# Layer 0 of a two-layer transformer step: layer-norm and turning of rows by pairs of tiles, row sums tied to the end of a head group, and a new order of three small steps

## The chip, the cores and the metric

The kernel runs on one core of a Trainium2 chip. The metric is the time of one execution in device microseconds (us); smaller is better. The engines are named as the profile names them: PE (matrix multiplication), PEld (its weight loads), DVE (vector), ACT (activation), POOL (the general engine), SP (here only an issuer of DMAs). Every engine runs its own list of instructions in the order in which the program has them, and waits on semaphores for the others.

## The reference

Eight sequences of 512 rows of 512 float32 numbers go through two layers. Cut to what matters here:

```python
x = layernorm(x + attention0(x))     # 16 heads of 32, causal, with biases
x = layernorm(x + experts(x))        # 8 experts, top 2 of a softmax router, low-rank additions to all weights
x = layernorm(x + attention1(x))     # 8 heads of 64, 2 groups of keys and values, RMS-scaled input
x = layernorm(x + ffn(x))            # 1408 hidden, integer weights with scales

def layernorm(x, eps=1e-5):
    return (x - mean(x)) / sqrt(var(x) + eps)

# the router of the experts
probs = softmax(x @ (gate_w + 2 * lora_B @ lora_A).T)
weights, selected = top_k(probs, 2);  weights = weights / weights.sum(-1)
```

## The kernel before

**Layer 0 (the first 650 us).** `attention0` loops over the batches `b` (the eight sequences), in each over four groups `g` of four heads, and in each over three units `u` of keys (key tile 0; tiles 1 and 3; tile 2). One step `(g, u)` multiplies scores (`sc`), takes their exponential on ACT (`p`, L1573), masks the diagonal block on POOL (`select`, L1583), and one step later multiplies by the values (`av`, L1612) and adds up `p` on DVE (L1620). The sums of `p` are multiplied by ones (`rs`), inverted, and `normalise` writes `aoT` (L1634).

**Work laid between the steps.** `plan(b)` gives each step `(g, u)` a list `todo`, which runs between the scores and the product, and a list `late`, which runs after the product:

- queries and keys of the next group (`query`, `key`);
- for the batch before, `pb = b - 1`: `project(pb, t)` for four tiles of rows, with the addition to `x` out of the bank (L1495), statistics (L200, L201), then the norm of four tiles (L205) with their four stores into the router's rows (SP, L208);
- for `pb` from 0 to 5 (`by_dma`): `blocks(pb)`, which transposes 32x32 blocks of the four normed tiles on DVE (L108), writes them to DRAM in four DMAs (`turns.out`, L113) and reads them back in one (`turns.back`, L116); the result `x1T` is what the router's logits multiply (`score`, at step (3, 2); L515), after which `choose` picks two experts of each row;
- for `b + 1`: the values in seven products of half-size blocks instead of eight (`ps_1of` to `ps_7of`, in the order 1, 6, 2, 5, 3, 7, 4; the last one is in the plan of the next batch), whose results DVE adds up (L1437). Some of them need differences of blocks of x, four additions over 128x512 in all, made by `row_sums` on DVE (L806), from the transposed x that SP loads into `experts` (`load_xT`, L1373).

**Merging.** Beside this the low-rank additions are merged into the experts' weights: at the third unit of a group SP loads two pieces of weights (`merged<-in_gate_up` or `merged<-in_down`, L853), POOL adds the scaled product to each in the next two units (L855), and SP stores them (L856). The loading of `x` and `xT` for the next batch and the merging in the last group are put behind the return `x1T<-turned` in the program (`behind_return`).

**What sets the order.** Within layer 0 a list scheduler orders the instructions of every engine by their dependences and its own costs; `tc.issue_after(i)` keeps what is built under it behind instruction `i`. In the last two groups of the last batch, PE's order is the program's own. In the program that comes out, the orders on SP and POOL are plain lists, and a DMA or an addition that waits holds up everything behind it on its queue.

**Banks.** The PSUM (the memory of matmul results) gives four banks to `sc`, two to `av` and two, tag `mm`, to everything else in layer 0: queries, keys, projections, seven-products, `rs`, logits and rank.

**The change of layer.** Before layer 1 the experts' tiles run on PE with pieces of the first attention of layer 1 laid between them: `first_pieces` of `Attention1`, whose last three are the key, the value and the first query.

Of the kernel before, what the change touches and what calls it, by code (L numbers as in the profile page):

```python
# [9 lines left out]
F32 = mybir.dt.float32  # L10
# [4 lines left out]
ALU = mybir.AluOpType  # L15
# [3 lines left out]
P = 128  # L19
# [3 lines left out]
NT = S // P  # L23
# [5 lines left out]
LN_EPS = 1e-5  # L29
# [407 lines left out]
class Router:  # L437
# [80 lines left out]
    def choose(self, b, parts, ps, columns):  # L518

        nc, small = self.nc, self.small  # L520
        here = slice(NT * b, NT * (b + 1))

        def bc(a):
            return a[:, :, None].to_broadcast([P, NT, E])

        for t in range(NT):
            matmul_by_columns(nc, ps[:, t, :], parts[:, ts(t, P)], self.gather, columns=columns)
        pr = small.tile([P, NT, E], F32, name="pr")
        tmp = small.tile([P, NT, E], F32, name="tmp")
        top = small.tile([P, NT], F32, name="top")  # L530
        second = small.tile([P, NT], F32, name="second")
        red = small.tile([P, NT], F32, name="red")
        total = small.tile([P, NT], F32, name="total")
        nc.vector.tensor_reduce(red, ps, AX.X, ALU.max)
        nc.vector.tensor_tensor(tmp, ps, bc(red), ALU.subtract)
        nc.scalar.activation(tmp, tmp, AF.Exp)
        nc.vector.tensor_reduce(red, tmp, AX.X, ALU.add)
        nc.vector.reciprocal(red, red)
        nc.vector.tensor_tensor(pr, tmp, bc(red), ALU.mult)

        def first_of_largest(values, largest, one_hot):
            nc.vector.tensor_reduce(largest, values, AX.X, ALU.max)
            nc.vector.tensor_tensor(tmp, values, bc(largest), ALU.is_equal)
            nc.vector.tensor_tensor(tmp, tmp, self.iota, ALU.mult)
            nc.vector.tensor_reduce(red, tmp, AX.X, ALU.min)
            nc.vector.tensor_tensor(one_hot, self.iota, bc(red), ALU.is_equal)

        first_of_largest(pr, top, self.hots[:, 0, here, :])

        rest = small.tile([P, NT, E], F32, name="rest")  # L550
        nc.vector.scalar_tensor_tensor(rest, self.hots[:, 0, here, :], -2.0, pr, ALU.mult, ALU.add)
        first_of_largest(rest, second, self.hots[:, 1, here, :])
        nc.vector.tensor_tensor(total, top, second, ALU.add)
        nc.vector.reciprocal(total, total)
        nc.vector.tensor_tensor(self.weights[:, 0, here], top, total, ALU.mult)
        nc.vector.tensor_tensor(self.weights[:, 1, here], second, total, ALU.mult)


        self.both = small.tile([P, NT, E], F32, name="both")
        nc.vector.tensor_tensor(self.both, self.hots[:, 0, here, :], self.hots[:, 1, here, :], ALU.add)  # L560
        self.earlier = small.tile([P, NT, E], F32, name="earlier")
        nc.vector.tensor_copy(self.earlier[:, 0, :], self.carry)
        for t in range(1, NT):
            nc.vector.tensor_tensor(self.earlier[:, t, :], self.earlier[:, t - 1, :], self.both[:, t - 1, :], ALU.add)
        nc.vector.tensor_tensor(self.carry, self.earlier[:, NT - 1, :], self.both[:, NT - 1, :], ALU.add)

    def dispatch(self, b, ps, columns):

# [242 lines left out]
class Experts:  # L811
# [9 lines left out]
    def room(self, at, n):  # L821

        return self.w[:, at : at + n * 512].rearrange("p (u f) -> p u f", f=512)
# [510 lines left out]
def attention0(env, guard, keep, routes, experts, dram, p_mm, tiles_ctx):  # L1334
# [4 lines left out]
    tc, nc, ins, xs, vec = env.tc, env.nc, env.ins, env.xs, env.vec  # L1339
# [4 lines left out]
    with ExitStack() as phase:  # L1344
# [47 lines left out]
        router = Router(env, keep, routes, small, work, dram)  # L1392
# [29 lines left out]
        def row_sums(b):  # L1422
            return seven_of_rows(nc, xts[b], t_x)

        def seven(b, n):
            x_of, _ = row_sums(b)
            room = v_rooms[b % 2]
            ps = mm([P, 2, 256], f"ps_{n}of7")
            for s in range(2):
                for k in range(2):  # L1430
                    matmul_by_columns(nc, ps[:, s, :], x_of[n][:, k, ts(s, P)], v_of[n][:, k, :], start=k == 0, stop=k == 1)

            def block(i, j):
                return room[:, 2 * j : 2 * (j + 1), 256 * i : 256 * (i + 1)]

            def add(out, a):
                nc.vector.tensor_tensor(out, ps, a, ALU.add)  # L1437

            if n == 1:
                nc.scalar.copy(block(0, 0), ps)  # L1440
            elif n == 6:
                add(block(1, 0), block(0, 0))
            elif n == 2:
                add(block(0, 0), block(0, 0))
            elif n == 5:
                add(block(1, 1), block(1, 0))
            elif n == 3:
                add(block(0, 1), block(1, 1))
            elif n == 7:
                add(block(1, 1), block(1, 1))  # L1450
                add(block(1, 0), block(1, 0))
            else:
                add(block(1, 0), block(1, 0))
# [37 lines left out]
        def project(b, t, out_of_heads=False):  # L1491
            ps = mm([P, D], "ps_o")
            for c in range(ND):
                (wide if out_of_heads else multiply)(ps, aoTs[b][:, c, ts(t, P)], wo[:, c, :], c)
            nc.vector.tensor_tensor(xs[b][:, t, :], ps, xs[b][:, t, :], ALU.add)  # L1495
            if t == NT - 1:
                env.layernorm(b, lambda t: router.rows[router.row_at(b, t) :][:P])

        x1Ts, logits = {}, {}

# [1 line left out]
        turns = Turn(env, dram, NT, "turned0")  # L1502
        returned = [None]
# [4 lines left out]
        def room(b):  # L1508
            x1Ts[b] = work.tile([P, ND, S], F32, tag="x1T", name="x1T")

        def blocks(b):
            room(b)
            flat = x1Ts[b].rearrange("p k s -> p (k s)")
            for t in range(NT):
                turns.blocks(flat, t, xs[b][:, t, :])
            turns.out(flat)
            returned[0] = turns.back(flat)

        def turn(b, c, mm=mm):
            if c == 0:  # L1520
# [119 lines left out]
        merging, inverses, normed = {}, [], [None]  # L1640
# [6 lines left out]
        def plan(b):  # L1647

            todo, late = ({(g, u): [] for g in range(ND) for u in range(len(UNITS))} for _ in range(2))
# [8 lines left out]
            pb, last = b - 1, b == NB - 1  # L1658
            by_dma = 0 <= pb < by_blocks
# [5 lines left out]
            if b:  # L1665
                places = ((1, 0), (1, 1), (1, 2), (2, 0)) if by_dma else ((1, 0), (1, 0), (1, 1), (1, 1) if last else (1, 2))
                for t, slot in enumerate(places):
                    todo[slot].append(lambda t=t: project(pb, t))
                if by_dma:
                    todo[2, 1].append(lambda: blocks(pb))  # L1670
                else:
                    for c in range(ND):
                        at = todo[2, 1] if last and c >= 2 else (late if last else todo)[2, 0]
                        at.insert(c % 2 if at is todo[2, 1] else len(at), lambda c=c: turn(pb, c))
                todo[(3, 2) if by_dma else (2, 1)].append(lambda: score(pb))
                if not by_dma:
                    todo[(3, 0) if last else (2, 2)].append(lambda: choose(pb))
            if b == 0:
                todo[1, 0].append(lambda: router.merge_lora(mm([P, ND, E], "ps_wr")))
            if b + 1 < NB:  # L1680
                for slot, last_sums in (((0, 2), False), ((1, 0), True)) if b else (((2, 1), False), ((2, 2), True)):
                    late[slot].append(lambda last_sums=last_sums: row_sums(b + 1)[1](last_sums))
                for n, slot in zip(ORDER, ((1, 0), (2, 0), (2, 1), (2, 2), (3, 0), (3, 2)) if b else
                                   ((3, 0), (3, 0), (3, 1), (3, 1), (3, 2), (3, 2))):
                    todo[slot].append(lambda n=n: seven(b + 1, n))
# [14 lines left out]
        tiles = Tiles(env, router, experts.w, dram)  # L1700
# [22 lines left out]
        for b in range(NB):  # L1723
            todo, late = plan(b)
# [41 lines left out]
        b = NB - 1  # L1766
# [28 lines left out]
class Attention1:  # L1795
# [83 lines left out]
    def first_pieces(self):  # L1879

        do = self.first = self.prepare(0)

        def fetch(t):
            do["fetch"](t)
            self.scale(t)

        def blocks(tiles):
            for t in tiles:
                do["blocks"](t)

        return ([lambda t=t: fetch(t) for t in range(NT)] + [lambda t=t: do["add"](t) for t in range(NT)]
                + [do["deviations"], do["norm"], lambda: blocks((0, 1)), lambda: blocks((2, 3)), lambda: None, lambda: None]
                + [do["key"], do["value"], lambda: do["query"](0)])

    def scale(self, c):

# [554 lines left out]
```

## Time and profile before

| | |
|---|---|
| time, median of 3 runs | 2086.05 us (2085.02 to 2086.63) |
| the profiled execution's own time | 2084.99 us |
| its span, first to last instruction | 2083.3 us |
| granted PE clock over the span | 0.998 |
| PE busy | 2058.4 us (99%) |
| DVE, ACT, POOL busy | 1264.3, 645.3, 510.7 us |
| layer 0's attention, to the first matmul of the experts | about 654 us |

The span is what the rows of the profile cover; 1.7 us of the execution lie around it. A row of the timeline gives the start in us, the time that the group of equal instructions took, the engine, the line, the operation, out<-in, shapes, the count, and in brackets how long the engine had been idle and what ended that. An SP row is an issue of a DMA, not its landing. PE's times overlap, as matmuls are pipelined, so that a start is a surer number than an end.

### The profile page before, as it was taken

To read this page: it belongs to the slowest core of one execution; us is meant where nothing else is said; L and a number is where in the kernel's file an instruction comes from. 1 tells how busy PE (TensorE), PEld (TensorE's weight loads), DVE (VectorE), ACT (ScalarE), POOL (GpSimd) and SP (SyncE) were. 2 spreads that over 40 slices of the span, in tenths; PEclk is the share of its full clock that TensorE was granted. 3 is DMA by queue.
4 is the path that set the end of the run, shared out by engine and by line. 5 is a ranking of instruction groups with operands and counts; after the bars stand their busy time and mean duration, and the time that the engine had idled before them with its cause. 6 is when DMAs were issued, how large, how long until landed. Compare 5 with 4: busy or idle time off the path is not lost. (4 is left out here: it accounts for less than half of the span.)

```text
span 2083.3 us, 37551 instructions
## 1 busy us (share of the span) xinstructions
PE 2058.4 (99%) x15778; PEld 1069.4 (51%) x15778; DVE 1264.3 (61%) x2047; ACT 645.3 (31%) x916; POOL 510.7 (25%) x509
## 2 busy tenths in 40 slices
PE   9999999999999999999999999999999999999998
PEld 2333333333334677764433333333335888888886
DVE  3667687686777533233158889887868644455444
ACT  2444434344344111111143333333332322222222
POOL 1344444444435121221052231232101000000000
PEclk9999999999999999999999999999999999999999
DMA  6023424415334488876432332223102311111000
GB/s 208 22 83 123 143 81 145 150 63 173 107 139 177 153 222 256 245 228 187 129 102 62 112 122 71 77 96 102 41 1 71 101 41 61 61 61 61 21 21 22
DMA packets 193059, 226.10 MB, mean 109 GB/s; under 512 B 73818, under 2 KB 139610, under 8 KB 189298
## 3 DMA queue, kind: packets, MB, share of 16 engines
q1 hardware_dynamic: 180240, 185.44, 28.3%
q0 software_dynamic: 10560, 34.61, 5.7%
q10 hardware_dynamic: 2082, 3.56, 0.6%
q8 instruction: 127, 2.08, 0.4%
q14 instruction: 50, 0.41, 0.1%
HBM read 138.88 MB, written 84.69 MB: 107 GB/s over the span
## 5 line engine op out<-in xcount | busy, mean ns | idle before, releaser
L1573 ACT ACTIVATE p<-sc 128x2048 f32<-128x2048 f32 (+1 forms) x96 | 152.4, 1587 | 175.8 <-PE sc L67 175.8
L1262 DVE SCALAR_TENSOR_TENSOR hT<-ps_u,vec,sg 128x512 f32<-128x512 f32 x88 | 65.6, 745 | 189.4 <-PE ps_u L1257 189.1
L1583 POOL TENSOR_SCALAR_AFFINE_SELECT p<-p 128x512 f32<-128x512 f32 x128 | 97.2, 771 | 307.6 <-ACT p L1573 302.0
L1273 PE MATMUL ps_f<-ffn_w,h_half 128*128 128x512 f32 x664 | 167.6, 393 | 2.8 <-DVE h_half L1268 2.0
L990 PE MATMUL ps_gu<-xrT,experts 128*128 128x256 f32 x736 | 166.6, 379 | 0.0
L1110 POOL TENSOR_TENSOR g_total<-g_total,r_inv 128x512 f32<-128x512 f32 x64 | 83.7, 1308 | 316.2 <-DVE r_inv L2007 270.6
L1620 DVE TENSOR_TENSOR p<-p 128x1536 f32<-128x1536 f32 (+2 forms) x96 | 147.8, 1539 | 17.7 <-POOL x L1593 10.0
L990 PEld LDWEIGHTS ps_gu<-xrT,experts 128*128 128x128 f32 x736 | 139.3, 190 | 35.9 <-issue 19.3
L1977 ACT ACTIVATE p<-sc 128x1024 f32<-128x1024 f32 x128 | 124.2, 1022 | 100.5 <-PE sc L67 99.2
L2007 DVE RECIPROCAL r_inv<-r_inv 128x512 f32<-128x512 f32 x32 | 107.1, 3347 | 71.6 <-ACT r_inv L1107 71.6
L1273 PEld LDWEIGHTS ps_f<-ffn_w,h_half 128*128 128x128 f32 x664 | 122.9, 188 | 34.5 <-DVE h_half L1268 7.4
L1257 PE MATMUL ps_g<-x_high,ffn_w 128*128 128x512 f32 x352 | 137.2, 390 | 0.0
L1257 PE MATMUL ps_g<-x_low,ffn_w 128*128 128x512 f32 x352 | 137.0, 389 | 0.0
L1257 PE MATMUL ps_u<-x_low,ffn_w 128*128 128x512 f32 x352 | 136.9, 389 | 0.0
L1257 PE MATMUL ps_u<-x_high,ffn_w 128*128 128x512 f32 x352 | 136.9, 389 | 0.0
L67 PE MATMUL ps_q<-experts 128*32 128x512 f32 x1024 | 120.1, 603 | 6.1 <-DMA experts<-in_xT 4.3
L67 PE MATMUL sc<-qT,kT 64*64 64x512 f32 x1024 | 124.7, 602 | 1.2 <-ACT qT L1871 0.9
L1260 ACT ACTIVATE sg<-ps_g,vec 128x512 f32<-128x512 f32 x88 | 60.6, 689 | 195.6 <-PE ps_g L1257 195.6
L1996 PE MATMUL av<-p,v 128*64 128x512 f32 x512 | 120.8, 593 | 0.0
L202 POOL TENSOR_SCALAR rstd<-mv 128x4 f32<-128x4 f32 x15 | 3.9, 262 | 461.9 <-DVE mv L201 461.9
L67 PE MATMUL ps_k<-experts 128*32 128x512 f32 x1024 | 116.4, 595 | 0.0
L67 PE MATMUL ps_o<-attn_out,aoT 128*64 128x512 f32 x512 | 116.4, 598 | 0.0
(310 smaller groups left out, 3419.2 us busy)
## 6 DMA issues: line engine op xcount, KB each, us to landing
results<-y SPq DMA_DIRECT2D x68, 256.0 KB, 2.6
pair<-xrT SPq DMA_DIRECT2D x30, 512.0 KB, 3.3
xrT<-pair SPq DMA_DIRECT2D x120, 128.0 KB, 3.9
turned<-turned SPq DMA_DIRECT2D x56, 256.0 KB, 4.1
merged<-merged SPq DMA_DIRECT2D x48, 256.0 KB, 2.4
experts<-merged SPq DMA_DIRECT2D x8, 1536.0 KB, 6.6
x<-in_x SPq DMA_DIRECT2D x8, 1024.0 KB, 8.4
merged<-in_gate_up SPq DMA_DIRECT2D x32, 256.0 KB, 3.9
```

Source lines behind the costliest of these rows:

```text
L67: nc.tensor.matmul(out[m], lhsT=lhsT[:, m], rhs=rhs, start=start, stop=stop)
L990: nc.tensor.matmul(ps[:, j, :], lhsT=w, rhs=xT[:, c, :], start=c == 0, stop=c == ND - 1)
L1110: self.nc.gpsimd.tensor_tensor(self.total, self.total, r_inv, ALU.add)
L1257: nc.tensor.matmul(ps, lhsT=w[:, ts(dc, P)], rhs=x[:, dc, :], start=(dc, i) == (0, 0), stop=(dc, i) == (ND - 1, 1))
L1262: nc.vector.scalar_tensor_tensor(hT, u, vec[:, V_SU + c : V_SU + c + 1], sg, ALU.mult, ALU.mult)
L1273: self.nc.tensor.matmul(os[t], lhsT=h[:, ts(t, P)], rhs=self.weights(2 * NHID + c), start=(c, i) == (0, 0), stop=(c, i) == (NHID - 1, 1))
L1573: nc.scalar.activation(p, sc[:, :, :width], AF.Exp, scale=scale)
L1583: select = nc.gpsimd.affine_select(out=first, in_=first, pattern=[[0, 4], [1, P]], compare_op=ALU.is_ge, fill=0.0, base=0, channel_multipl ...
L1620: nc.vector.tensor_tensor(total[:, :, P * kt :], total[:, :, P * kt :], p[:, :, at : at + w], ALU.add)
L1977: nc.scalar.activation(p, sc, AF.Exp, scale=scale)
L1996: nc.tensor.matmul(st["av"][HD * j : HD * (j + 1), :], lhsT=st["v"][:, kt, HD * j : HD * (j + 1)], rhs=p[:, j, :], start=kt == 0, stop=kt ...
L2007: nc.vector.reciprocal(r_inv, r_inv)
```

## The change

Six things are edited.

1. `project` in layer 0 takes the statistics of each tile itself and, after the last tile, computes the inverse deviations. `layernorm` is not called there any more except for the last batch's projection.
2. The norm, `norm_rows`, is made by pairs of tiles and built behind the last addition out of a bank that was built before it (`behind_add`, with `added[0]`): tiles 0 and 1 in the `late` list of step (2, 0), tiles 2 and 3 in that of (2, 1). Where `x` isn't turned by DMA, both pairs are in `late` of (1, 1).
3. `blocks` is made by pairs too, in the same way: tiles 0 and 1 in `late` of (2, 1), 2 and 3 in `late` of (2, 2); the DMAs out and back follow the second pair. It was in `todo` of (2, 1).
4. The sums of x for the next batch's seven products are built behind the last `aoT` that was built (`normed[0]`).
5. In `choose` the weights of the two experts are computed after the counts that the ranks need.
6. In layer 1's first pieces the query comes before the value.

```diff
@@ choose
-        nc.vector.tensor_tensor(total, top, second, ALU.add)
-        nc.vector.reciprocal(total, total)
-        nc.vector.tensor_tensor(self.weights[:, 0, here], top, total, ALU.mult)
-        nc.vector.tensor_tensor(self.weights[:, 1, here], second, total, ALU.mult)
...
         nc.vector.tensor_tensor(self.carry, self.earlier[:, NT - 1, :], self.both[:, NT - 1, :], ALU.add)
+        nc.vector.tensor_tensor(total, top, second, ALU.add)
+        nc.vector.reciprocal(total, total)
+        nc.vector.tensor_tensor(self.weights[:, 0, here], top, total, ALU.mult)
+        nc.vector.tensor_tensor(self.weights[:, 1, here], second, total, ALU.mult)
@@ attention0
+        def sums_of_rows(b, last):
+            with tc.issue_after(normed[0].ins):
+                row_sums(b)[1](last)
...
             def add(out, a):
-                nc.vector.tensor_tensor(out, ps, a, ALU.add)
+                added[0] = nc.vector.tensor_tensor(out, ps, a, ALU.add)
...
-            nc.vector.tensor_tensor(xs[b][:, t, :], ps, xs[b][:, t, :], ALU.add)
+            added[0] = nc.vector.tensor_tensor(xs[b][:, t, :], ps, xs[b][:, t, :], ALU.add)
+            if out_of_heads:
+                if t == NT - 1:
+                    env.layernorm(b, lambda t: router.rows[router.row_at(b, t) :][:P])
+                return
+            if t == 0:
+                stats[:] = env.small.tile([P, NT, 6], F32, name="stats"), env.small.tile([P, NT, 2], F32, name="mv")
+            nc.vector.bn_stats(out=stats[0][:, t, :], in_=xs[b][:, t, :])
+            nc.vector.bn_aggr(out=stats[1][:, t, :], in_=stats[0][:, t, :])
             if t == NT - 1:
-                env.layernorm(b, lambda t: router.rows[router.row_at(b, t) :][:P])
+                rstd = env.small.tile([P, NT], F32, name="rstd")
+                nc.gpsimd.tensor_scalar(rstd, stats[1][:, :, 1], LN_EPS, None, ALU.add)
+                nc.gpsimd.tensor_tensor(rstd, rstd, env.neg_half, ALU.pow)
+                stats.append(rstd)
+
+        def norm_rows(b, *tiles):
+            for t in tiles:
+                x = xs[b][:, t, :]
+                nc.vector.tensor_scalar(x, x, stats[1][:, t, 0:1], stats[2][:, t : t + 1], ALU.subtract, ALU.mult)
+                nc.sync.dma_start(out=router.rows[router.row_at(b, t) :][:P], in_=x)
+
+        def behind_add(thunk):
+            with tc.issue_after(added[0].ins):
+                return thunk()
...
-            for t in range(NT):
+            for t in tiles:
                 turns.blocks(flat, t, xs[b][:, t, :])
-            turns.out(flat)
-            returned[0] = turns.back(flat)
+            if tiles[-1] == NT - 1:
+                turns.out(flat)
+                returned[0] = turns.back(flat)
@@ plan
+                for tiles_of, slot in zip(((0, 1), (2, 3)), ((2, 0), (2, 1)) if by_dma else ((1, 1), (1, 1))):
+                    late[slot].append(lambda tiles_of=tiles_of: behind_add(lambda: norm_rows(pb, *tiles_of)))
                 if by_dma:
-                    todo[2, 1].append(lambda: blocks(pb))
+                    late[2, 1].append(lambda: behind_add(lambda: blocks(pb, 0, 1)))
+                    late[2, 2].append(lambda: behind_add(lambda: blocks(pb, 2, 3)))
...
-                    late[slot].append(lambda last_sums=last_sums: row_sums(b + 1)[1](last_sums))
+                    late[slot].append(lambda last_sums=last_sums: sums_of_rows(b + 1, last_sums))
@@ first_pieces
-                + [do["key"], do["value"], lambda: do["query"](0)])
+                + [do["key"], lambda: do["query"](0), do["value"]])
```

What the scheduler makes of it: the orders of instructions on SP and POOL are the same as before. On DVE, in each of the six batches that are turned by DMA, the run "four norms, four transposes, addition of `ps_2of`" becomes "two norms, addition of `ps_2of`, two norms, two transposes", and the other two transposes stand behind the addition of `ps_5of`, which is the seventh instruction after the first two. The four sums of x stand behind the `aoT` of the previous batch's last group, which comes at step (0, 1) (three, then the addition over 128x1024 of `p`, then one), where before two of them stood ahead of the additions of `p` at the end of the batch and two between the seven-products' additions. The instructions of `choose` stand in the same order as before. On PE the first query of layer 1 and the value change places, the last of the value's sixteen matmuls standing behind the branch that ends the tiles; on ACT the two copies out of their banks change places too.

More of the change, by code (lines that the diff above doesn't have):

```diff
@@ L1494, in project @@
                 (wide if out_of_heads else multiply)(ps, aoTs[b][:, c, ts(t, P)], wo[:, c, :], c)
-            nc.vector.tensor_tensor(xs[b][:, t, :], ps, xs[b][:, t, :], ALU.add)
-            if t == NT - 1:
-                env.layernorm(b, lambda t: router.rows[router.row_at(b, t) :][:P])
+            added[0] = nc.vector.tensor_tensor(xs[b][:, t, :], ps, xs[b][:, t, :], ALU.add)
[7 more added lines that the diff above has]
+            nc.vector.bn_aggr(out=stats[1][:, t, :], in_=stats[0][:, t, :])
+            if t == NT - 1:
+                rstd = env.small.tile([P, NT], F32, name="rstd")
[10 more added lines that the diff above has]
+                return thunk()
+        stats, added = [], [None]
         x1Ts, logits = {}, {}
@@ L1509, in room, with blocks @@
             x1Ts[b] = work.tile([P, ND, S], F32, tag="x1T", name="x1T")
-        def blocks(b):
-            room(b)
+        def blocks(b, *tiles):
+            if tiles[0] == 0:
+                room(b)
             flat = x1Ts[b].rearrange("p k s -> p (k s)")
-            for t in range(NT):
+            for t in tiles:
                 turns.blocks(flat, t, xs[b][:, t, :])
-            turns.out(flat)
-            returned[0] = turns.back(flat)
+            if tiles[-1] == NT - 1:
+                turns.out(flat)
+                returned[0] = turns.back(flat)
         def turn(b, c, mm=mm):
```

## Prediction

> **What bounds the kernel now.** I read the page first, then PE's waits, then the timelines of DVE, SP, POOL and PE over one batch of layer 0 (that with `pb` = 4, from 467 to 515 us), then the share of the DMAs in that stretch.
>
> ```profile
> span 2083.3 us, 37551 instructions
> PE 2058.4 (99%) x15778; PEld 1069.4 (51%) x15778; DVE 1264.3 (61%) x2047; ACT 645.3 (31%) x916; POOL 510.7 (25%) x509
> ...
> PE ps_q L67 <- DVE experts L1437: 1.4, 2, 1.0
> PE sc L67 <- ACT p L1573: 1.2, 1, 1.2
> PE sc L67 <- ACT qT L1871: 0.9, 1, 0.9
> ```
>
> PE is the bound: all its idle time is 25 us, some 9 of them after 2050 us. The change's parts can reach three waits: `ps_q` for a bank that DVE frees late (1.4 us in two batches), and layer 1's first scores for `qT` (0.9). So it can win 2.3 us at most, and it loses whatever it makes PE wait anew. The question is what it makes late.
>
> ```profile
> 472.12 2.23 DVE L205 TENSOR_SCALAR x<-x,mv,rstd 128x512 f32<-128x512 f32 x4 [1.48 <-POOL rstd L203]
> 474.27 2.47 DVE L108 STREAM_TRANSPOSE x1T<-x 128x512 f32<-128x512 f32 x4
> 476.68 0.65 DVE L1437 TENSOR_TENSOR experts<-ps_2of,experts 128x512 f32<-128x512 f32 x1
> ...
> 484.51 0.69 DVE L1437 TENSOR_TENSOR experts<-ps_5of,experts 128x512 f32<-128x512 f32 x1 [0.19 <-PE ps_5of L67]
> ...
> 499.56 1.42 DVE L806 TENSOR_TENSOR experts<-experts 128x512 f32<-128x512 f32 x2 [7.15 <-DMA experts<-in_xT]
> ```
>
> DVE's part: the four transposes end at 476.75. DVE is idle before 499.56 because it waits for `xT` with the sums of x.
>
> ```profile
> 476.78 3.78 SPq L113 DMA_DIRECT2D turned<-x1T  x4
> 485.35 0.33 SPq L116 DMA_DIRECT2D x1T<-turned  x1
> 485.78 0.39 SPq L1377 DMA_DIRECT2D x<-in_x  x1
> 486.22 1.41 SPq L856 DMA_DIRECT2D merged<-merged  x2
> 487.67 0.47 SPq L1373 DMA_DIRECT2D experts<-in_xT  x1
> 495.05 1.41 SPq L853 DMA_DIRECT2D merged<-in_gate_up  x2
> ```
>
> SP issues in this order, and all of it hangs on the transposes: four DMAs out at once after them, the return 8.6 us later when they have landed, then x (1 MB), two stores, `xT` (1 MB). The loads L853 wait at 495.05 for the stores, which landed behind x.
>
> ```profile
> 506.40 3.49 POOL L855 TENSOR_TENSOR merged<-merged,scaled 128x512 f32<-128x512 f32 x2
> 509.85 1.09 POOL L1583 TENSOR_SCALAR_AFFINE_SELECT p<-p 128x512 f32<-128x512 f32 x1
> ...
> 499.39 1.06 PE L515 MATMUL ps_logits<-x1T,r_wr 128*32 128x512 f32 x8
> 508.78 3.64 PE L67 MATMUL ps_q<-experts 128*32 128x512 f32 x32 [1.01 <-DVE experts L1437]
> 512.24 1.04 PE L1612 MATMUL av<-p,experts 128*32 128x512 f32 x8
> ```
>
> Two consumers close the chain: PE's logits at 499.39 need the return; POOL's additions L855 at 506.40 need the two loads, and behind them in POOL's list stands the mask of `p` that PE's `av` at 512.24 reads.
>
> ```profile
> 477.00:485.30 8.30, 8.30 (x132) 3.29 (x126) 7.64 (x8) 4.38 (x8) 4.27 (x3) 1.00 0.62 129
> 485.30:494.00 8.70, 8.70 (x133) 3.34 (x136) 1.44 (x2) 2.64 (x2) 2.03 (x3) 1.00 0.82 265
> 494.00:501.00 7.00, 7.00 (x100) 2.45 (x96) 1.41 (x3) 4.24 (x7) 2.48 (x3) 1.00 1.07 400
> ```
>
> The last two columns (DMA share, GB/s) say that after the return's issue the engines are nearly full: what hangs behind it doesn't catch up.
>
> **The change, part by part.**
>
> *Pairs of norms and transposes (six batches).* No instruction is added; the second pair of transposes moves behind the addition of `ps_5of`. I replay DVE's new list on the durations above. The norms begin at 472.12 as before (rstd is there), two end by 473.3. The addition of `ps_2of` waits for its product: PE starts it at 474.47, and 1.98 us from start to DVE's start is what `ps_5of` shows (482.53 to 484.51), so 476.45. Then, start to start: addition 0.61, two norms of 0.54, two transposes of 0.60, to 479.3. Additions of `p` (1.67 and 0.61) with the inverse's two steps between (0.61 and 0.72) to 482.9; `aoT` 0.61; `p` over 128x1024 1.80 (it took 2.18 in this batch); so `ps_5of` at about 485.5 instead of 484.51, and the last transpose ends at about 487.3. That is 10.6 us after 476.75. It can't be under 9.65: 485.20, where the addition of `ps_5of` ends at the earliest, and two transposes. The other five batches have the same distances to 0.05 us.
>
> The out and return DMAs, x, stores, `xT` and L853 all start 10.6 us later. Is there that much room? From the trace, by batch (return landed / logits start; first L853 landed / POOL's addition / mask ended / `av` start):
>
> 0: 162.06 / 171.79; 172.00 / 178.19 / 182.72 / 184.02
> 1: about 243.6 / 254.02; 253.55 / 259.88 / 264.43 / 265.78
> 2: 325.49 / 335.79; about 335.4 / 341.30 / 345.83 / 347.55
> 3: 407.36 / 417.56; about 417.2 / 423.56 / 428.10 / 429.39
> 4: 490.17 / 499.39; 500.27 / 506.40 / 510.94 / 512.24
> 5: 572.41 / 582.24; 580.59 / 586.37 / 590.47 / 594.00
>
> ("About": the landing isn't in the trace; taken from the neighbours' time from issue.) The return's room is 9.2 to 10.4 us, less than 10.6: PE waits 0.3 to 1.5 us at the logits, 4.6 in all. The loads' room is 5.8 to 6.4, so POOL's additions wait 4.2 to 4.8 us, and the mask and `av` with them. New `av` start = landing + 10.6 + (mask ended - addition started: 4.5, in batch 5 4.1) + 0.1 for the semaphore: 187.2, 268.8, 350.6, 432.4, 515.5, 595.4; against before: 3.2, 3.0, 3.1, 3.0, 3.3, 1.4, sum **17.0**. The logits' 4.6 lie inside this: PE comes that much later to `av`, and the loads don't. Queued behind the waiting additions are only masks, whose `p` PE wants later than this one. The out transfers took 7.4 to 8.6 us; without the stores of rows beside them they may all take the short time: **-1**.
>
> What I cost at nothing: the two later row stores (SP has nothing before the transposes, POOL's gather of rows is far off); the later `aoT` (+1.4 us; its bank is wanted a group later); the later `ps_5of` (+1.0; its bank is wanted by `ps_3of` at 489.74); x for the next batch (10.6 later than 494.06; POOL wants it at 515.2); `xT` (now at 510.2, wanted by the sums at about 521). Without these covers each costs its own lateness.
>
> *Sums of x behind `aoT`.* The four take 3.7 us of DVE either way. Ahead of 508.78 DVE no longer waits for `xT`, so `ps_q` finds its bank free: -1.0 here, -0.4 in batch 0. Both are already inside the 17.0, which counts from the old starts. In the new place they stand ahead of the addition of `ps_o`, whose bank `ps_rank` wants. DVE's list there was 25 us without a pause because it started late; starting earlier, it reaches that addition about 1 us before the bank is wanted. Between 0 and +1 us a batch; I take 0, as the wait for `av` gives DVE more time still.
>
> *Choice.* The order of instructions stays as it was: 0.
>
> *First query of layer 1.* It removes 0.86 us of PE's wait for `qT`, since ACT copies it 12 us earlier. In its place one matmul of the value (0.2 us) waits behind the branch; ACT's copy of the value (0.59) stands before the first exponential, while PE multiplies scores for 2 us. The branch's cost to PE isn't in the trace: between 0 and the 0.86 itself. I take half: **-0.5**.
>
> *The clock.* PE's first 32 matmuls of `ps_q` took 5.41 us where later ones take 3.64: after idleness PE starts slow, 1.8 us lost. [...]
>
> Sum: 17.0 - 1 - 0.5 = +15.5. On the profiled execution's 2084.99 that is 2100.5; the median is 1.1 above it, so **2101.5 us**.
>
> **The rivals.**
>
> *Only the return counts* (+2.6): if the loads L853 landed early enough that POOL doesn't wait, but the return comes late, PE loses 4.6 at the logits and wins 1.5 and 0.5: 2088.7. For: the loads are 0.5 MB only. Against: they stand behind 2 MB at 0.8 and more of the engines.
>
> *The chain catches up* (-2, not slower): one mechanism, the DMAs from the out transfers to L853. Before they take 23.5 us (476.78 to 500.27). If they took 4.8 us less, lateness at POOL would be within its 5.8, the return with it, and only the savings remain: 2084. For: stores and `xT` are issued without waiting for POOL. Against: the share of 0.82 to 1.07.
>
> [...]
>
> **How the numbers follow.** The main case 0.74, with own bounds from +10 (9.65 us late, all sizes favourable) to +21 (POOL's additions and `ps_o` at their worst); only the return 0.10; catching up 0.08; the clock 0.05; 0.03 for a gain over 0.2% that I can't name, as 2.3 us is all that the waits hold. 0.2% is 4.2 us, about what a measurement of this kernel can tell from no change. Slower: 0.74 + 0.05 + 0.03 of the return's case = 0.82; same: the rest of that case and catching up, 0.15; faster 0.03. The range from 2090 to 2108 leaves out catching up, most of the clock's case and about a tenth of the main one's ends.
>
> **What would show it.** PE's waits should name the logits behind `x1T<-turned` and `av` behind POOL's mask or its release, 2 to 3 us in each of five batches; SP's issue of the return 10 us later against the addition of `ps_5of` than now; POOL's L855 idle before it on `merged<-in_*`. I am wrong if L855 at the head of a batch still starts at once behind the sum of inverses L1110, or if the logits don't wait.

## The result: 24.8 us slower

The changed kernel took 2110.38 us (median of 4 runs, 2109.74 to 2111.03) where the kernel before took 2085.55 beside it (4 runs, 2085.02 to 2086.63): +24.8 us, ratio 1.0118, 95% interval 1.0105 to 1.013. The forecast was +15.5 us, 2101.5, with a range up to 2108. The sign and the main mechanism were right, the size was not, and the time lies 2.4 us outside the range.

The profiled execution of the changed kernel took 2111.03 us, 26.0 more than that of before. The page's head and the rows of PE's waits that are new (line, what is waited for: us in total, times, longest):

```profile
span 2109.3 us, 37558 instructions
PE 2064.0 (98%) x15778; PEld 1071.9 (51%) x15778; DVE 1281.6 (61%) x2047; ACT 647.7 (31%) x916; POOL 501.2 (24%) x509
...
PE ps_rank L67 <- DVE x L1497: 7.6, 4, 2.1
PE av L1639 <- POOL p L1610: 7.3, 5, 3.4
...
PE ps_logits L515 <- DMA x1T<-turned: 2.6, 4, 1.1
PE ps_logits L515 <- ACT scaled L844: 2.4, 1, 2.4
PE ps_logits L515 <- ACT r_rough L79: 1.0, 1, 1.0
```

The waits at the logits and at `av` are the two that were forecast. (Two of the logits' rows name ACT, the semaphore that came last by the profile. Both are the return: in all six batches the logits start 5.0 to 5.3 us after SP issues it.) The wait of `ps_rank` on the addition out of `ps_o`'s bank is the largest, and it was forecast as nothing.

The chain of DVE, SP, POOL and PE in the batch that the prediction shows (`pb` = 4):

```profile
498.20 1.00 DVE L1515 TENSOR_SCALAR x<-x,mv,rstd 128x512 f32<-128x512 f32 x2
499.11 1.30 DVE L108 STREAM_TRANSPOSE x1T<-x 128x512 f32<-128x512 f32 x2
...
506.66 0.68 DVE L1439 TENSOR_TENSOR experts<-ps_5of,experts 128x512 f32<-128x512 f32 x1
507.26 1.29 DVE L108 STREAM_TRANSPOSE x1T<-x 128x512 f32<-128x512 f32 x2
```
```profile
508.58 3.79 SPq L113 DMA_DIRECT2D turned<-x1T  x4
516.50 0.33 SPq L116 DMA_DIRECT2D x1T<-turned  x1
...
526.00 1.16 SPq L851 DMA_DIRECT2D merged<-in_gate_up  x2
```
```profile
531.31 2.51 POOL L853 TENSOR_TENSOR merged<-merged,scaled 128x512 f32<-128x512 f32 x2 [6.59 <-DMA merged<-in_gate_up]
533.78 1.83 POOL L1610 TENSOR_SCALAR_AFFINE_SELECT p<-p 128x512 f32<-128x512 f32 x3
...
521.64 1.06 PE L515 MATMUL ps_logits<-x1T,r_wr 128*32 128x512 f32 x8 [1.03 <-ACT r_rough L79]
...
534.46 1.07 PE L1639 MATMUL av<-p,experts 128*32 128x512 f32 x8 [0.87 <-POOL p L1610]
```

PE is 21.1 us behind the kernel before at this point. The out transfers started at 476.78 there and at 508.58 here: 31.8 later, less 21.1, is 10.7 us late against PE's work. The forecast was 10.6. POOL, which started its additions at once before, now stands idle 6.59 us for the loads. In this batch the chain is as forecast; what differs is the price.

To see where PE falls behind, I align PE's groups of matmuls of two traces and list the places where the difference of their starts jumps (left out are jumps below 0.25 us, and PE's first matmuls, whose wait for the first load differs from one execution to another, 4.3 to 4.6 us by the waits). Sums in us over the batches, for the changed kernel and for the experiments that follow (the clock and layer 1 are told further down):

| kernel against before | logits | `av` | `ps_q` | `ps_rank` | half clock | layer 1 |
|---|---|---|---|---|---|---|
| forecast | 17.0 for these three together, -1 | | | 0 | 0 | -0.5 |
| changed kernel | +6.5 | +8.3 | -1.55 | **+8.4** | **+2.7** | +1.2 |
| pairs of norms and turns only | +5.2 | +13.3 | -1.55 | 0 | 0 | 0 |
| sums of x only | 0 | 0 | -1.55 | +4.9 | 0 | 0 |
| changed, last group not loaded | +5.2 | 0 | -1.55 | +3.9 | 0 | +2.6 |
| changed, four tiles behind `ps_2of` | 0 | 0 | -1.55 | +5.6 | 0 | +2.0 |
| changed, sums behind `ps_o`'s additions | +5.8 | +9.0 | -1.55 | 0 | +2.9 | +2.8 |
| four tiles and sums so, value first | 0 | 0 | -1.55 | 0 | 0 | 0 |

The jumps of the changed kernel add up to 25.6 of its 26.0 us. Each row is one profiled execution, not the median of its kernel: that execution took 2.3 us more than the median with the last group not loaded, 1.9 more with four tiles behind `ps_2of`, and 1.8 less with pairs only.

### The profile page after: what moved, and what is told of

Its sections match the earlier page's. It is cut to its first block, busy times and chain, and to the rows that moved or that the text cites. A ratio compares the mean times of both kernels' runs of the same rounds, so it can differ in the third digit from the quotient of the medians.

```text
span 2109.3 us, 37558 instructions
## 1 busy us (share of the span) xinstructions
PE 2064.0 (98%) x15778; PEld 1071.9 (51%) x15778; DVE 1281.6 (61%) x2047; ACT 647.7 (31%) x916; POOL 501.2 (24%) x509
## 5 line engine op out<-in xcount | busy, mean ns | idle before, releaser
L67 PE MATMUL ps_q<-hT,attn_qkv 128*64 128x512 f32 (+1 forms) x504 | 116.2, 596 | 0.0
```

The source lines that it names most:

```text
L67: nc.tensor.matmul(out[m], lhsT=lhsT[:, m], rhs=rhs, start=start, stop=stop)
```

## Experiments

Medians below are each beside runs of the kernel before on the same chip: 2085.73 us for pairs only, sums only, the last group not loaded and four tiles behind `ps_2of`; 2086.75 for the sums with POOL's additions left out, the query only, the changed kernel with the sums behind `ps_o`'s additions, and the first kernel of "Towards a faster one"; 2085.90 for the rest. After the result I held that the pairs cost about what was forecast and that the sums of x, which now start earlier, cost the rest by meeting POOL's additions on DVE; the rivals were that they cost by their place in DVE's list alone, and that POOL's late additions do it all. The letters in the quoted expectations belong to the question of each run.

### Each part alone

**Pairs of norms and turns only.** From the changed kernel:

```diff
-                    late[slot].append(lambda last_sums=last_sums: sums_of_rows(b + 1, last_sums))
+                    late[slot].append(lambda last_sums=last_sums: row_sums(b + 1)[1](last_sums))
...
-                + [do["key"], lambda: do["query"](0), do["value"]])
+                + [do["key"], do["value"], lambda: do["query"](0)])
```

> Only the norms and transposes by pairs (and the statistics in project); the sums of x, the choice and layer 1's order are as before. Theory A (the return chain): the second transposes make the out and return DMAs, x, stores, xT and the merging's loads some 10.6 us late. The sums of x stand at their old place in DVE's list and wait for that late xT, in front of the additions that free PE's banks, so PE's ps_q waits for DVE by some 9 us in each of the five batches with an xT load, in place of the 2 us that the masks cost: slower than before by 45 to 60 us. Theory B (the two moves are independent: the pairs cost the logits and av waits, the sums the rank wait): slower by about 14 us, ps_rank without a wait.

Measured: 2105.14 us, +19.4, ratio 1.0097 (1.0081 to 1.0112). PE's waits, and POOL's additions in the second batch:

```profile
PE av L1639 <- POOL p L1610: 12.2, 5, 3.0
PE ps_logits L515 <- DMA x1T<-turned: 3.9, 5, 1.0
...
268.88 3.26 POOL L853 TENSOR_TENSOR merged<-merged,scaled 128x512 f32<-128x512 f32 x2 [6.49 <-DMA merged<-in_gate_up]
```

No row of `ps_rank` on `x` is left, and in this execution the clock stays whole. The other three executions had a lower mean clock (0.996 and 0.997 against 0.999) and took 1.7 to 4.1 us longer. That would fit drops of the clock like those described further down, but no trace of them was kept. The sums of x don't stand in front of additions that free a bank that PE soon wants: three of the four run from 268.04, where DVE waited 3.36 us for `xT`, while PE waits for POOL's mask anyway. The case of 45 to 60 us is out. Logits, `av` and `ps_q` make 5.2 + 13.3 - 1.55 = 17.0 us, the first term of the forecast to the tenth, though not batch by batch (see the table under "Why the prediction was right and wrong").

**Sums of x only.** The kernel before with the sums built behind `normed[0]`:

```diff
+        def sums_of_rows(b, last):
+            with tc.issue_after(normed[0].ins):
+                row_sums(b)[1](last)
...
-                    late[slot].append(lambda last_sums=last_sums: row_sums(b + 1)[1](last_sums))
+                    late[slot].append(lambda last_sums=last_sums: sums_of_rows(b + 1, last_sums))
```

> Only the sums of x behind aoT. Theory A: the wait of ps_rank came from POOL's late additions, which stretched the choice on DVE and ran beside the sums; without the late chain the additions come early, the wait is 0 to 1 us a batch, ps_q's 1.4 us are gone: between 1.5 us faster and 4 us slower than before. Theory B: the place of the sums alone costs ps_rank its 2 us in four to six batches, 8 us, less the 1.4: about 7 us slower.

Measured: 2088.89 us, +3.2, ratio 1.0015 (1.0006 to 1.0024). `ps_q` wins the 1.55 us back, `ps_rank` loses 1 us in each of five batches. Its wait, then DVE and POOL at the same time:

```profile
PE ps_rank L67 <- DVE x L1499: 4.0, 5, 0.8
...
273.58 4.71 DVE L806 TENSOR_TENSOR experts<-experts 128x512 f32<-128x512 f32 x3
...
273.09 1.28 POOL L1110 TENSOR_TENSOR g_total<-g_total,r_inv 128x512 f32<-128x512 f32 x1 [0.69 <-DVE r_inv L81]
274.32 3.42 POOL L855 TENSOR_TENSOR merged<-merged,scaled 128x512 f32<-128x512 f32 x2
```

A sum takes 1.57 us here on average. Where no addition of POOL runs beside it, it takes 0.68 (the row `L804 ... x1` of the changed kernel at 285.84, below). In the new place three of them meet three additions of POOL, one of the sum of inverses and two of the merging, and both engines give way: POOL's two take 3.42 us instead of 2.51.

**Sums of x only, POOL's additions beside them left out.** The kernel with the sums only, without the merging additions of the first group (two of the three that the sums met; the merged weights lack them):

```diff
-        return {0: load, 1 + i: lambda: nc.gpsimd.tensor_tensor(w[0], w[0], scaled, ALU.add),
+        return {0: load, 1 + i: lambda: nc.gpsimd.tensor_tensor(w[0], w[0], scaled, ALU.add) if k % ND else None,
```

> Only the sums of x behind aoT, and POOL leaves out the merging's additions of each batch's first group (those pieces of the merged weights lack their low-rank part). Theory A': the three sums take 4.7 us instead of 1.8 because POOL's sum of inverses and its two additions, released by the same inverse, run beside them; without the additions the sums take under 3.2 us, ps_rank's wait of 1.0 a batch is gone: 1.5 us faster than before. Rival: the sums are slow by their place in DVE's list alone, or the wait is the list's length: the sums' time or the wait stays, 3 us slower as e2.

Measured: 2086.16 us, -0.6, ratio 1.0 (0.999 to 1.0009). The same three sums:

```profile
273.47 2.54 DVE L806 TENSOR_TENSOR experts<-experts 128x512 f32<-128x512 f32 x3
```

2.54 us instead of 4.71, and PE's wait of `ps_rank` on `x` is gone from the list. So the sums' cost is the meeting with POOL, not their place in DVE's list as such. (The 1.5 us of gain that were expected lie inside the interval, but aren't shown.)

**Query before value only.** The kernel before with the last two pieces of layer 1's first projections changed over.

> Only layer 1's first query before the value. The prediction's step: half of the 0.86 us wait for qT is won, 0.5 us faster. Rival: three of the five runs so far have the query first, and all three show an idle time of 1.4 to 2.9 us of PE before the third group of layer 1's scores, while none of the others does; then 0.3 us are won and 1 to 3 lost: 1 to 2.5 slower than before.

Measured: 2089.76 us, +3.0, ratio 1.0017 (1.0008 to 1.0026). The wait of 0.86 us at layer 1's first scores is gone (the second row shows the 0.30 us that the value's last matmul waits behind the branch), but another one comes 9 us later. PE, then ACT:

```profile
1047.84 1.17 PE L67 MATMUL ps_v<-attn_qkv,hT 128*128 128x128 f32 x9
1049.30 0.46 PE L67 MATMUL ps_v<-attn_qkv,hT 128*128 128x128 f32 x2 [0.30 <-PEq L1074]
...
1053.91 3.65 PE L67 MATMUL ps_q<-hT,attn_qkv 128*64 128x512 f32 x16
1057.39 1.89 PE L1996 MATMUL av<-p,v 128*64 128x512 f32 x8
1062.27 1.95 PE L67 MATMUL sc<-qT,kT 64*64 64x512 f32 x16 [2.99 <-ACT qT L1871]
...
1061.63 0.58 ACT L1871 COPY qT<-ps_q 128x512 f32<-128x512 f32 x1 [6.12 <-remote]
```

The second query's last matmul ends at about 1057.6 by the profile, and ACT had been idle since 1055.5. Its copy waits for PE's semaphore alone, which came at 1061.6. In the kernel before the same copy starts within 0.1 us of that end. I see no instruction between the two that would explain 4 us. The ends of matmuls are modelled in the profile, so the matmul itself may have ended late.

**Query, key, value; and value, key, query.** Two other orders of the three pieces, one execution each.

> The kernel before with the pieces of layer 1's first projections in the order query, key, value. Theory A (the gap before the third group of scores comes with value standing last, whose last matmul then stands behind the branch): gap of about 3 us, 2.5 to 3 us over the kernel before. Theory B (the gap comes with query standing between key and value): no gap, within 1 us of the kernel before.

> The kernel before with these pieces in the order value, key, query: query last as in the kernel before, another order of the rest. Theory A (value last makes the gap): no gap. Theory B (any other order of these pieces than the kernel before's moves what follows): a gap of 1 us or more before the third group of scores.

Measured: 2084.64 and 2085.30 us, single executions without an interval; no gap in either. PE in the first:

```profile
1056.37 1.89 PE L1996 MATMUL av<-p,v 128*64 128x512 f32 x8
1058.18 1.95 PE L67 MATMUL sc<-qT,kT 64*64 64x512 f32 x16
```

Here too the value stands last, with its last matmul behind the branch, and PE starts the third group of scores without a wait. So neither that matmul nor the query before the value makes the gap: only the order key, query, value showed it, with 1.5 to 3.1 us in all six kernels that have it. What delays PE's semaphore there stays open.

### Undoing the costs in the changed kernel

**Last group not loaded.** The changed kernel, without the loads L851 of the last group, on which POOL's late additions hang; the additions stay, and that group is merged without its base.

```diff
-            nc.sync.dma_start(out=w[0], in_=src.rearrange("e p f -> p e f"))
+            if k % ND < ND - 1:
+                nc.sync.dma_start(out=w[0], in_=src.rearrange("e p f -> p e f"))
```

> The changed kernel, but the merging in the last group of each batch leaves out its two loads L853; POOL adds the scaled product to itself instead (these pieces of the merged weights are not the right ones). POOL's additions then wait for no load. Theory A: av's waits for the mask (8.3 us) and the clock's drop after the longest of them go, ps_rank's waits (8.4) fall below 3, the logits' waits for the return stay at 4 to 6: 5 to 9 us slower than before instead of 25. Theory B: av's waits go, ps_rank's stay at 8: 14 to 17 slower.

Measured: 2095.13 us, +9.4, ratio 1.0044 (1.0029 to 1.006).

```profile
PE ps_logits L515 <- DMA x1T<-turned: 4.4, 5, 1.1
PE ps_rank L67 <- DVE x L1498: 3.1, 4, 0.8
```

The waits of `av` are gone, so they do hang on the loads behind the return. The logits' remain (5.2 us by the starts). `ps_rank` falls from 2 us a batch to 1, as with the sums alone (3.9 us in all by the starts, where the expectation had less than 3, and the whole is 0.4 us over its upper end). So of its 8.4 us about half is the sums beside POOL's additions after `aoT`; the other half comes with POOL's late additions. The trace of the changed kernel shows how: they run from 268.13 to 270.6, beside DVE's choice of experts, and two of its steps, 0.19 us each in the kernel before, take six times as long, which is the 1.27 us of the POOL addition that each stands behind. From its first step to the copy of the counts the choice takes 9.0 us, 7.3 before:

```profile
268.13 2.51 POOL L853 TENSOR_TENSOR merged<-merged,scaled 128x512 f32<-128x512 f32 x2 [5.97 <-DMA merged<-in_gate_up]
...
268.18 1.27 DVE L546 TENSOR_TENSOR r_hots<-r_iota,red 128x32 f32<-128x32 f32 x1
269.49 1.20 DVE L551 SCALAR_TENSOR_TENSOR rest<-r_hots,pr 128x32 f32<-128x32 f32 x1
...
279.03 0.69 DVE L1661 TENSOR_TENSOR aoT<-av,r_inv 128x512 f32<-128x512 f32 x1
279.64 4.71 DVE L804 TENSOR_TENSOR experts<-experts 128x512 f32<-128x512 f32 x3
284.27 1.65 DVE L1647 TENSOR_TENSOR p<-p 128x1024 f32<-128x1024 f32 x1
285.84 0.68 DVE L804 TENSOR_TENSOR experts<-experts 128x512 f32<-128x512 f32 x1
286.45 0.68 DVE L1497 TENSOR_TENSOR x<-ps_o,x 128x512 f32<-128x512 f32 x1
...
287.18 0.29 PE L67 MATMUL ps_rank<-both,r_before 128*32 128x32 f32 x8 [2.13 <-DVE x L1497]
```

From `aoT` on, DVE's list is one unbroken row up to the addition that PE waits for, so what it lost before `aoT` (1.7 us here) is not made up, and PE's wait is about 1 us longer than with the sums alone.

**Four tiles behind `ps_2of`.** The changed kernel, with all transposes again ahead of `ps_5of`'s addition:

```diff
-                    late[2, 1].append(lambda: behind_add(lambda: blocks(pb, 0, 1)))
-                    late[2, 2].append(lambda: behind_add(lambda: blocks(pb, 2, 3)))
+                    late[2, 1].append(lambda: behind_add(lambda: blocks(pb, 0, 1, 2, 3)))
```

> The changed kernel, but all four transposes follow the second pair of norms, behind the addition of ps_2of, instead of two behind that of ps_5of. They end about 3.9 us later than before instead of 10.6, under the loads' room of 5.8 and the return's of 9.2. Theory A: no waits of the logits for the return nor of av for the mask; ps_rank at 0 to 1 a batch: between 2 us faster and 4 slower than before. Theory C (pairs as such cost, by DVE's order or its port, not by the return): 10 or more slower still.

Measured: 2089.68 us, +3.95, ratio 1.0018 (1.0008 to 1.0027). Neither a logits nor an `av` wait is left: the second pair's place is the whole cause of both. What remains is the sums (`ps_rank` +5.6) and the gap in layer 1.

**Sums behind `ps_o`'s additions.** The changed kernel, with the sums of batches 2 to 6 behind the additions of tiles 1 and 2 instead of ahead of tile 0's:

```diff
-            with tc.issue_after(normed[0].ins):
+            with tc.issue_after((added[0] if b > 1 else normed[0]).ins):
...
-                for slot, last_sums in (((0, 2), False), ((1, 0), True)) if b else (((2, 1), False), ((2, 2), True)):
+                for slot, last_sums in (((1, 1), False), ((1, 2), True)) if b else (((2, 1), False), ((2, 2), True)):
```

> The changed kernel, but the sums of x stand behind the additions of the second and third ps_o (steps (1, 1) and (1, 2)) instead of behind aoT. If ps_rank's 8.4 us in the changed kernel need the sums ahead of ps_o's addition, all of it goes and the chain's waits (logits and av, about 13 to 17 us net, with or without a drop of the clock) stay: 13 to 19 us slower than before. If the late additions of POOL alone made it, 4 us of it stay: 18 to 22 slower.

Measured: 2103.56 us, +16.8, ratio 1.0081 (1.0066 to 1.0097). `ps_rank` doesn't wait any more, while logits and `av` still do. The late additions of POOL alone therefore cost `ps_rank` nothing, here as with pairs only; the sums in the new place alone cost 4.9 us; the two together cost 8.4.

### Towards a faster one

**The kernel before, sums behind `ps_o`'s additions, query before value.**

> Before, with the sums of x behind the additions of the second and third ps_o, and the query first in layer 1; no pairs. ps_q's waits of 1.5 us go, no chain is late, ps_rank doesn't wait; the query's part wins 0.3 or loses 1 to 3 as e5 will tell: between 2 faster and 1.5 slower than before.

Measured: 2087.97 us, +1.2, ratio 1.0006 (0.9997 to 1.0015). No wait of `ps_rank`, and 1.55 us less of `ps_q`; but the gap in layer 1 takes 3.04 us, and 1.42 of half clock come behind it.

**The same, value before query.**

> The kernel before with one edit: the sums of x of batches 2 to 6 stand behind ps_o's additions of tiles 1 and 2 of their step; queries, norms and turns as before. Theory (the sums cost only where they meet POOL's additions, and query first costs about 3 us by itself): no ps_rank wait, ps_q waits shorter by 1.5 us together, no wait of 3 us before layer 1's third group of scores, so 1.5 us under the kernel before, ratio 0.9993. Rival (the sums were as well placed before; what the shorter ps_q waits give comes back elsewhere): 1.0000.

Measured: 2083.89 us, -2.0, ratio 0.9991 (0.9982 to 1.0).

**The changed kernel without its three costs:** four tiles behind `ps_2of`, sums behind `ps_o`'s additions, value before query.

> The changed kernel with its three costs taken out together: all four tiles turned behind ps_2of's addition, the sums of x behind ps_o's additions of tiles 1 and 2, value before query. Theory: no logits wait, no av wait, no ps_rank wait; what is left are the shorter ps_q waits, so the same as the run beside it (about 2084 to 2085 us, 1.5 under the kernel before). Rival (statistics by tile and norms behind additions cost by themselves): 2 us or more above it.

Measured: 2084.11 us, -1.8, ratio 0.9991 (0.9982 to 1.0). In both traces, apart from an offset out of the first matmuls (PE waited 4.5 us for the first load, 4.3 before), PE's starts differ from those of before by the two waits of `ps_q` alone, -0.47 and -1.08 us. That accounts for 1.55 us of the gain. The gain is of the size of 0.1%, and its interval ends at 1.0, so it is just about at the limit of what can be told from none. The two kernels lie 0.2 us apart, so statistics by tile and norms behind additions cost nothing that shows.

## Why the prediction was right and wrong

- **The late transposes: right.** 10.6 us late by replaying DVE's list, 10.7 measured. Logits and `av` waited where they were said to. POOL's idle time names `merged<-in_gate_up` or `merged<-in_down` in five batches, and in batch 2 another load, `lora<-in_lora`.
- **The sum of 17.0: 3.7 too high in the changed kernel, and two of its terms mis-sized.** Logits, `av` and `ps_q` together, by batch, in us:

| | 0 | 1 | 2 | 3 | 4 | 5 | sum |
|---|---|---|---|---|---|---|---|
| forecast | 3.2 | 3.0 | 3.1 | 3.0 | 3.3 | 1.4 | 17.0 |
| pairs only | 3.3 | 3.3 | 3.9 | 3.8 | 2.2 | 0.5 | 17.0 |
| changed kernel | 2.0 | 1.5 | 4.2 | 4.0 | 1.1 | 0.5 | 13.3 |

  The first term is "mask ended - addition started: 4.5", with 0.1 for the semaphore. It was taken from before, where POOL's two additions took 3.49 us. With the sums of x moved away from them they take 2.51 in all five batches that have such a wait, and from their start to `av` it is 3.15 us (531.31 to 534.46); with pairs alone 4.4 in four of the five. The same collision was in the old number, and one edit of the change removed it. This is 1.4 us a batch, more than the whole difference.

  The second term is that the DMAs between the out transfers and POOL's start would keep their old times. In the changed kernel that way took 24.8 and 24.6 us in batches 2 and 3, where 22.2 and 22.3 were forecast. In batch 2 the two loads took 7.7 us from issue to POOL's start, against 4.1 to 5.6 in batches 0, 1, 3 and 4. There SP issues four more loads (`lora<-in_lora`) right behind them, at 351.42, where the kernel before issued these 4.6 us after the first one (335.52 after 330.96). That these slowed them wasn't tested. So the terms erred in opposite directions, and that pairs alone met 17.0 to the tenth is in part luck.
- **"-1" for shorter out transfers: not seen.** Out to return took 7.92 us here (8.57 before), but in the batch before it 9.4 (420.74 to 430.12), which made the one logits wait of 2.5 us and the larger part of that batch's excess. Why it was slow there isn't settled.
- **"I take 0" for the sums behind `aoT`: the step that failed, +8.4.** It was bounded at 0 to +1 us a batch. The durations were those of the old place, 3.7 us for the four. In the new one three of them lie beside POOL's additions and take 4.71. The trace of before gave the hint: a sum at 262.13 took 1.80 us beside POOL's additions, while two additions out of a bank beside them took 0.68 each:

```profile
259.88 3.51 POOL L855 TENSOR_TENSOR merged<-merged,scaled 128x512 f32<-128x512 f32 x2
...
260.94 1.28 DVE L1437 TENSOR_TENSOR experts<-ps_7of,experts 128x512 f32<-128x512 f32 x2
262.13 1.80 DVE L806 TENSOR_TENSOR experts<-experts 128x512 f32<-128x512 f32 x1
```

  So not every DVE instruction was held up beside POOL's additions: the two with one operand in a bank stayed at 0.68 us, and the sum, with none there, did not. In the changed kernel the choice's two steps at 268.18 and 269.49 start 0.05 and 0.12 us behind a POOL addition and end 0.05 us behind it. The second half of the 8.4, POOL's late additions across the choice, is the same meeting, and the upper bound of 1 us a batch lacked it. The remark that the wait for `av` gives DVE time held in one batch of five: behind the `av` wait of 3.6 us `ps_rank` waited 0.
- **The clock at 0: wrong, +2.7.** The clock was halved twice. Here are the stretches ahead of the first drop and within both (PE busy second; the granted clock before the last two columns):

```profile
286.00:287.30 1.30, 0.12 (x12) 0.12 (x16) 1.26 (x3) 0.00 (x0) 0.00 (x0) 1.00 0.87 195
287.30:290.70 3.40, 3.40 (x60) 1.32 (x61) 3.26 (x20) 0.22 (x1) 0.00 (x0) 0.50 0.25 80
...
362.40:365.80 3.40, 3.40 (x44) 1.08 (x40) 3.30 (x3) 2.03 (x5) 1.06 (x1) 0.50 0.51 155
```

  Each drop lasted 3.41 us, and over each PE's starts fell 1.6 us further behind those of before, of which the table counts 1.35 to 1.4. One came after a wait of 2.13 us, one after 3.40; in the 3.41 us just ahead of each, PE was busy for 1.29. The forecast's sum has no term for the clock. The one slow start that it had from the trace of before is that of the first 32 matmuls, 5.41 us for 3.64, behind 4.33 us in which PE was idle. No run shows the size behind the chance of 0.05 for the clock's case; the runs showed these two drops, 2.9 us with the sums behind `ps_o`'s additions, and 1.4 in the first kernel of "Towards a faster one".
- **Query first at -0.5: wrong, +1.2** here (-0.25 and +1.47), +3.0 alone. The term itself came out at -0.26; the gap that stands 9 us behind it was not in it.
- **Choice at 0: right.** Its instructions kept their order.

Together: 13.3 + 8.4 + 2.7 + 1.2 = 25.6 against 16.0 + 0 + 0 - 0.5. The chance of 0.05 on the clock's case, and a main case whose own upper end was +21, made the range too short: two terms that were set at nothing and one that was set at a gain all came out as costs, and only the mis-sized sum took 2.7 us of that back (13.3 for 16.0).

## What to carry to other kernels

Before a DVE addition like the sums of x is moved, look at POOL's row for the new stretch as well as DVE's: beside POOL's additions a sum took 1.57 us instead of 0.68, and two of theirs 3.42 instead of 2.51, so its old duration is no price. When several edits are costed by one trace, recompute each duration that another edit's collision was part of; here one term fell by 1.4 us a batch and another rose by 2. And a chain that hangs transposes, a round trip through DRAM and loads on one queue should have its head moved only with the slack of every consumer in hand: 10.7 us of lateness against 9 to 10 and 6 of slack made the 13 to 17 us.

## What the runs showed of the hardware

- TensorE's clock was halved for 3.41 us after a wait of only 2.13 us; PE was busy for 1.29 of the 3.41 us ahead of that drop. Waits of about one length did not all end alike. An `av` wait of 3.0 us with pairs alone was followed by no drop (granted clock 0.999 over that execution); one of 3.2 us with the sums behind `ps_o`'s additions was followed by a granted clock of 0.61 over the next 3.4 us and 0.88 over the 3.3 behind them. The gap in layer 1 left 0.95 us of PE's work in 3.5 us in the first kernel of "Towards a faster one" (1055.5 to 1059), and the clock was 0.52 in the next 3.5; with the query first alone it left 0.78 (1058.5 to 1062), and the clock stayed at 1.00. What decides between them isn't shown. PE's busy time is modelled, so these figures are no finer than the profile.
- POOL's additions and DVE's sums of x took longer beside each other: 3.42 us instead of 2.51 for two on POOL, 1.57 on average instead of 0.68 for one on DVE. Two DVE steps of the choice, 0.19 us each in the kernel before, started 0.05 and 0.12 us behind a POOL addition of 1.27 us and took 1.27 and 1.20.
- A semaphore of PE came 4 us after the matmul that raises it ended by the profile (1061.6 after 1057.6, query first alone), in one order of instructions out of four tried. It is not explained.
